# Second graph stage: first maxima in five parts, Exp table earlier, 257 gathered columns, last rows stored from a tile of their own

## The chip, the cores and the metric

The kernel runs on one core of a Trainium2 chip. The core has five engines with instruction streams of their own: TensorE (PE in the profile; PEld is its loading of weights), VectorE (DVE), ScalarE (ACT), GpSimd (POOL) and SyncE (SP), which here only issues DMAs. Each engine takes its instructions in order; between engines semaphores hold an instruction back until what it needs is there. SBUF is the on-chip memory of 128 partitions, PSUM the accumulator memory that TensorE writes, DRAM the large memory. The metric is device time in microseconds (us), the median over runs; lower is better.

## The reference, cut to what matters

Two layers over x of 3327 rows and 256 features, each a graph stage and a feed-forward stage. The first layer is a normalised neighbour sum and a mixture of eight experts. The second layer is graph attention and multi-head attention with four heads and four expert queries each. The graph attention is the part that changes:

```python
Wh = x @ W                                # x: layer-normed rows, 3327 x 256
e_src = Wh @ a[:d_out]
e_dst = Wh @ a[d_out:]
e = jax.nn.leaky_relu(e_src[:, None] + e_dst[None, :], 0.2)
mask = (adj > 0) | jnp.eye(N, dtype=bool)
e = jnp.where(mask, e, NEG_INF)
alpha = jax.nn.softmax(e, axis=1)
h = alpha @ Wh
...
x = x + h
```

## The kernel before

Rows are padded to 3328 = 26 tiles of 128 (NT = 26, P = 128, NP = 3328, HP = 1664). Stages follow one another: `graph0` (first graph), `Experts.run` (experts), `graph1` (second graph), `heads` (attention and everything after it). Inside a stage the order of instructions on each engine is the order in which the program writes them (class InOrder, lines 50 to 99), so a waiting instruction holds all that is written behind it on its engine. Nearly all instructions pass through line 61, so the profile gives that line for them, and they are told apart by the names of their tiles. The SBUF pools of a stage take the space of pools that are closed, and a tile there waits for the last use of what lay there before; a DMA's use ends when it has landed.

`graph1` has two parts.

The first (lines 600 to 618) is a loop over k that takes the 26 row tiles through five steps, each with its own delay: `joined` (VectorE adds the experts' results to x and takes mean and variance, GpSimd makes the scale), `norm` (ScalarE), `turn` (TensorE transposes, ScalarE copies), `project` (TensorE) and `keep` (ScalarE copies to `wh` and `dst`). `gw` holds W and two further columns, W times each half of a, made once in `graph1_weights` (lines 404 to 446). So one matmul gives 258 columns: Wh, e_src, e_dst. `wh` is one tile of 26 times 259 columns, the last column being 1, so that the gathering also gives the softmax's denominator. `dst` holds e_dst plus a bound `shift`, spread over all partitions, 3328 columns.

The maximum of a row's masked e_dst is a product with `sg` (1 for a neighbour, 0 for none) that keeps the largest value: `top` (lines 518 to 528), an instruction on VectorE for each row tile and each part of the columns. PARTS (line 491) gives the bounds: for the first block of four tiles three parts, 1664, 1152 and 512 columns; for later blocks two of 1664. The first part runs inside the loop at k = 18, 20, 22 and 24, the second at k = 28 to 31, the third (line 743) after the loop, once the last tile's `dst` is there. At k = 30 (line 612) ScalarE runs an Exp on one column whose only purpose is to load the table of the exponential; it writes into a column of `own` (line 508), which line 736 then fills.

The second part goes through seven blocks of four row tiles, the last of two, and through 26 column tiles j in each, so 182 steps. `shifts` (line 626) reduces the parts' maxima of a block and makes two vectors a and b; `rows` spreads them by matmuls with ones, `spread_rows` copies them to `bc`. A step is `weights` (VectorE: u = max(a + d8, b); ScalarE: Exp), `masked` (VectorE: p = u where the panel `pan` of the adjacency matrix is set) and `gather` (TensorE: for each row tile, p times `wh[:, j, :]` into an accumulator of 259 columns). Two steps run ahead. In the first 16 steps of a block the next block's rows are turned to signs on ScalarE and their eight maxima taken on VectorE; at j = 16 `shifts` runs for the next block. `finish` (line 717) divides by the denominator, adds to x and stores the row tile to DRAM (`xs`); that DMA is issued by GpSimd. It runs for a block's tiles at the first steps of the next block, for the last block after all steps. GpSimd also sets the diagonal of each block's panel (`noti`, `ident`, line 681). `early` (line 753) runs the first three tiles of the attention's preparation inside the last blocks.

In `heads`, `prepare` and `heads_of` make the keys `kt`, queries `qt` (the first tiles: `qts`), the copy `sxd` and the values for one row tile; `v` and `xt` are tiles of the pool `self.work`, one buffer each. `v` is written to DRAM (`vs`) by four DMAs on SP in `keep_values`, and loaded again as `vr`. `mx` holds the maxima of a unit's scores; `sq` (line 1174) takes an output of ScalarE that is not used, beside the sum that is.

Of the kernel before, what the change touches and what calls it, by code (L numbers as in the profile page):

```python
# [12 lines left out]
F32 = mybir.dt.float32  # L13
BF16 = mybir.dt.bfloat16
# [3 lines left out]
AF = mybir.ActivationFunctionType  # L18
ALU = mybir.AluOpType
AX = mybir.AxisListType  # L20
# [81 lines left out]
class Net:  # L102
# [301 lines left out]
    def graph1_weights(self, pool):  # L404

        a = self.a

        self.gw = pool.tile([P, 2, D + 2], F32, name="gw")
        self.nc.scalar.dma_start(
            out=self.gw[:, :, :D], in_=a["gw"].rearrange("(k p) o -> p k o", p=P)  # L410
        )
        ga = pool.tile([P, 2 * D], F32, name="ga")
        self.nc.scalar.dma_start(out=ga, in_=a["ga"].partition_broadcast(P))
        self.vd = pool.tile([P, 2, P], F32, name="vd")
        self.shift = pool.tile([P, 1], F32, name="shift")
        self.noti = pool.tile([P, P], F32, name="noti")
        junk = pool.tile([P, D], F32, name="pj")

        def make(nc, ps):
            gw, shift = self.gw, self.shift  # L420
            nc.gpsimd.tensor_tensor(self.noti, self.ones, self.ident, ALU.subtract)
            for k in range(2):
                for i in range(2):
                    nc.vector.scalar_tensor_tensor(
                        junk, gw[:, k, :D], 1.0, ga[:, ts(i, D)], ALU.mult, ALU.mult,
                        accum_out=gw[:, k, D + i : D + i + 1],
                    )


            sq = junk[:, :2]  # L430
            nc.vector.tensor_tensor(sq, gw[:, :, D + 1], gw[:, :, D + 1], ALU.mult)
            nc.vector.tensor_copy(
                self.vd, gw[:, :, D + 1 : D + 2].to_broadcast([P, 2, P])
            )
            yield 1
            pv = ps()
            for k in range(2):
                nc.tensor.matmul(
                    pv[:, 0, :1], self.ones, sq[:, k : k + 1], start=(k == 0), stop=(k == 1)
                )  # L440
            nc.vector.tensor_scalar(shift, pv[:, 0, :1], 1e-30, None, ALU.max)
            nc.gpsimd.tensor_tensor(shift, shift, self.nhalf[:, :1], ALU.pow)
            nc.vector.reciprocal(shift, shift)
            nc.vector.tensor_scalar(shift, shift, 16.1, 1.0, ALU.mult, ALU.add)

        return make
# [37 lines left out]
    def graph1(self, xs, vs, made, pool):  # L484
# [3 lines left out]
        self.sxtp, self.sxts = pool, []  # L488
        HP = NP // 2

        PARTS = ((0, HP, HP + 9 * P, NP), (0, HP, NP))
        with ExitStack() as ctx:
            one = ctx.enter_context(tc.tile_pool(name="g1", bufs=1))
            panp = ctx.enter_context(tc.tile_pool(name="g1pan", bufs=3))
# [6 lines left out]
            W = D + 3  # L501
            wh = one.tile([P, NT, W], F32, name="wh")
            nc.gpsimd.memset(wh[:, :, D + 2 : W], 1.0)
            e_src, e_dst = wh[:, :, D], wh[:, :, D + 1]
            dst = one.tile([P, NP], F32, name="dst")
            d8 = one.tile([P, NT], F32, name="d8")
            d2 = one.tile([P, NT], F32, name="d2")
# [9 lines left out]

            def top(t, part, parts):

                if t not in tops:  # L520
                    tops[t] = s.tile([P, 3], F32, tag="gtop", name="gtop", bufs=8)[:, : len(parts) - 1]
                lo, hi = parts[part : part + 2]
                h = lo // HP
                sg = signs[t, h][:, lo - h * HP : hi - h * HP]
                nc.vector.tensor_tensor_reduce(
                    sg, sg, dst[:, lo:hi], 1.0, -3e38, ALU.mult, ALU.max,
                    tops[t][:, part : part + 1],
                )


# [71 lines left out]
            for k in range(NT + 6):  # L602
                if k + 6 < NT:
                    fetch(k + 6)

                for lag, work in ((0, joined), (2, norm), (3, turn), (4, project), (5, keep)):
                    if 0 <= k - lag < NT:
                        work(k - lag)
                for t in range(4):
                    if k == 18 + 2 * t:  # L610
                        top(t, 0, PARTS[0])
                if k == NT + 4:

                    nc.scalar.activation(own[:, 0:1], shift, AF.Exp, scale=-1.0)
                for t in range(4):
                    if k == 28 + t:
                        top(t, 1, PARTS[0])
            first.close()

            ep = ctx.enter_context(tc.tile_pool(name="g1e", bufs=4))  # L620
# [5 lines left out]
            def shifts(b):  # L626


                tiles = blocks[b]
                n, t0 = len(tiles), tiles[0]  # L630
                es = e_src[:, t0 : t0 + n]
                m = s.tile([P, 4], F32, tag="m", name="m")[:, :n]
                ab = s.tile([P, 2, 4], F32, tag="ab", name="ab")[:, :, :n]
                for i, t in enumerate(tiles):
                    nc.vector.tensor_reduce(m[:, i : i + 1], tops.pop(t), AX.X, ALU.max)
                nc.vector.tensor_tensor(m, m, own[:, t0 : t0 + n], ALU.max)
                nc.vector.scalar_tensor_tensor(m, m, shift, es, ALU.subtract, ALU.add)
                nc.vector.scalar_tensor_tensor(m, m, 0.2, m, ALU.mult, ALU.max)
                nc.vector.tensor_tensor(ab[:, 0, :], es, m, ALU.subtract)
                nc.vector.scalar_tensor_tensor(ab[:, 1, :], es, 0.2, m, ALU.mult, ALU.subtract)  # L640
                dg = abp.tile([P, 2, 4, P], F32, tag="dg", name="dg1")
                for i in range(2):
                    (nc.gpsimd if b else nc.vector).tensor_tensor(
                        dg[:, i, :n, :],
                        self.ident.unsqueeze(1).to_broadcast([P, n, P]),
                        ab[:, i, :].unsqueeze(2).to_broadcast([P, n, P]),
                        ALU.mult,
                    )
                return dg
# [57 lines left out]
            def gather(k):  # L707
                b, j = steps[k]
                p = ps_.pop(k)
                for i, t in enumerate(blocks[b]):  # L710
                    if j == 0:
                        accs[t] = psa.tile([P, W], F32, tag="acc", name="acc1")
                    nc.tensor.matmul(
                        accs[t], p[:, i, :], wh[:, j, :], start=(j == 0), stop=(j == NT - 1)
                    )

            def finish(t):
                ph = accs.pop(t)
                rd = s.tile([P, 1], F32, tag="rd", name="rd")
                nc.vector.reciprocal(rd, ph[:, D + 2 : W])  # L720
                nc.vector.scalar_tensor_tensor(
                    x[:, t, :], ph[:, :D], rd, x[:, t, :], ALU.mult, ALU.add
                )
                nc.gpsimd.dma_start(out=xs[ts(t, P), :], in_=x[:, t, :])

            groups = [(b, g) for b in range(len(blocks)) for g in range((NT + 3) // 4)]

# [12 lines left out]
                if k in when:  # L740
                    load(*when[k])
            for t in blocks[0]:
                top(t, 2, PARTS[0])
            spread_rows(0, rows(0, shifts(0)))
            for k in range(3):
                if k in when:
# [178 lines left out]
    def heads(self, xs, vs, out):  # L925
# [3 lines left out]
        with ExitStack() as ctx:  # L929
# [47 lines left out]
            def prepare(t, res):  # L977
# [40 lines left out]
                yield  # L1018

                pp = self.valued(nc, partial(ps.tile, [P, 2, P], F32, tag="b", name="pv"), sxt)  # L1020
                v = self.work.tile([P, D], F32, tag="v", name="v", bufs=1)
                empty(v.rearrange("p (c q) -> p c q", c=2), pp, D)
                yield
                yield from heads_of(t, res, sxt, nz, v)
# [94 lines left out]
            def drain(u, g):  # L1119

                n = span(u["t"], g)[1] * P
                last = g == u["t"] // 4
                if g == 0:
                    u["sc"] = {}
                    u["mx"] = sm.tile([P, 4, 8], F32, tag="mx", name="mx")
                sc = u["sc"][g] = scp.tile([P, 4, BLK], F32, tag="sc", name="sc")
                for e in range(4):
                    s, m = u["pq"][e][:, :n], u["mx"][:, e, g : g + 1]
                    if last:
                        nc.vector.tensor_tensor_reduce(  # L1130
                            sc[:, e, :n], s, mask[:, BLK - n :], 1.0, NEG, ALU.add, ALU.max, m
                        )
                    else:
                        nc.vector.tensor_scalar(
                            sc[:, e, :n], s, 1.0, None, ALU.mult, ALU.max, accum_out=m
                        )
                    load["dve"] += 0.12 + 0.00104 * n
                if last:
                    u["nmax"] = sm.tile([P, 4], F32, tag="nmax", name="anmax")
                    nc.vector.tensor_reduce(  # L1140
                        u["nmax"], u["mx"][:, :, : g + 1], AX.X, ALU.max, negate=True
                    )
                    load["dve"] += 0.2
# [27 lines left out]
                nc.vector.transpose(w, w)  # L1171
                load["dve"] += 0.1 + 0.00417 * n

            sq = one.tile([P, 64], F32, name="sq")


            po = ps_o.tile([P, 4, BLK], F32, tag="po", name="po")
# [973 lines left out]
```

## Time and profile before

Three runs took 2844.63, 2844.79 and 2849.79 us, median 2844.79. One more execution was profiled; it took 2842.88 us, of which 2840.9 lie between the first and the last instruction.

| stretch (us) | what runs | length | PE | DVE | ACT | POOL | PE clock |
|---|---|---|---|---|---|---|---|
| 0 to 69 | first graph: features | 69.0 | 49.3 | 36.6 | 42.4 | 41.6 | 0.97 |
| 69 to 384 | first graph: gathering, routing | 315.0 | 312.6 | 107.5 | 66.9 | 135.8 | 0.99 |
| 384 to 537 | experts | 153.0 | 130.2 | 54.2 | 77.1 | 68.7 | 0.93 |
| 537 to 598.5 | second graph: projecting | 61.5 | 48.5 | 51.3 | 37.2 | 48.2 | 0.87 |
| 598.5 to 611.7 | second graph: up to the first gathering | 13.2 | 3.8 | 7.9 | 5.0 | 0.0 | 0.58 |
| 611.7 to 967.8 | second graph: 182 steps | 356.1 | 323.0 | 340.2 | 191.7 | 89.2 | 0.99 |
| 967.8 to 2840.9 | attention and the rest | 1873.1 | 1786.5 | 1774.4 | 1370.7 | 694.1 | 0.99 |

The columns of the engines give busy time in the stretch; the last column is the clock that TensorE was granted, 1 being full speed. A busy share near the length of a stretch says that the engine may set its pace; what decides is who waits for whom. In lines of the timeline the numbers are start, length, engine, line, operation, output and input tiles, shapes, count, and in brackets how long the engine had stood before it and what ended that. In lines of the chain they are start, length and what held the end of the run there. An fp32 matmul shows as two records.

### The profile page before, as it was taken

How to read it: one execution, taken by the hardware profiler on the slowest of the kernel's cores; microseconds unless marked ns; L12 is line 12 of the kernel's file. 1: busy time of each engine (PE TensorE's matmuls, PEld its weight loads, DVE VectorE, ACT ScalarE, POOL GpSimd, SP SyncE). 2: the span in 40 equal slices, each digit the busy share in tenths (PEclk: the TensorE clock that was granted, in tenths of full speed). 3: DMA queues.
4: the chain of work that ended last, by engine and by line, in shares of the span. 5: the costliest groups of instructions: out<-in, count | busy, mean ns of one | idle time of the engine just before them, and what ended most of it. 6: DMA issues, size and time to landing. Idle time of an engine off the chain costs nothing.

```text
span 2840.9 us, 124987 instructions
## 1 busy us (share of the span) xinstructions
PE 2653.9 (93%) x53422; PEld 1970.7 (69%) x53422; DVE 2372.1 (83%) x5521; ACT 1790.9 (63%) x5131; POOL 1077.6 (38%) x1565
## 2 busy tenths in 40 slices
PE   7999988878988998999999999999999999999995
PEld 5888887756767776676666666666666666666664
DVE  5202643589999798999999999999999999999996
ACT  6520135555555467877777777777778777776774
POOL 5541644532133148655444333333233322223122
PEclk9999999989999899999999999999999999999998
DMA  9994568656785333434434443444434434444432
GB/s 379 386 339 138 191 212 281 202 188 238 277 285 174 94 91 88 117 109 112 119 108 117 118 116 114 119 120 121 115 115 116 126 116 124 123 117 117 116 106 80
DMA packets 257755, 449.29 MB, mean 158 GB/s; under 512 B 58768, under 2 KB 156176, under 8 KB 257072
## 3 DMA queue, kind: packets, MB, share of 16 engines
q1 hardware_dynamic: 245104, 417.11, 47.0%
q0 software_dynamic: 6576, 18.02, 1.7%
q8 instruction: 420, 6.88, 1.0%
q10 hardware_dynamic: 5520, 6.18, 0.6%
q14 instruction: 135, 1.11, 0.1%
HBM read 392.98 MB, written 25.88 MB: 147 GB/s over the span
## 4 chain that ended last, share of the span: by engine, by line
DVE 35%; PE 30%; ACT 4%; issue 2%; POOL 1%; DMA 0%; POOLq 0%; DVEq 0%; ACTq 0%
DVE sc L61 32%; PE pqk L61 11%; PE po L61 10%; PE acc L61 3%; ACT sc L61 2%; PE ptO L61 2%; PE pq L61 1%; PE psxt L61 1%; DVE p L61 1%; PE ph L61 0%; PE pk L61 0%; PE pt L61 0%; DVE sg L61 0%; ACT sq L61 0%; DVE u L61 0%
## 5 line engine op out<-in xcount | busy, mean ns | idle before, releaser
L61 ACT ACTIVATE sc<-sc,anmax 128x512 f32<-128x512 f32 (+3 forms) x1568 | 1041.4, 669 | 101.9 <-DVE anmax L61 101.8
L61 PEld LDWEIGHTS po<-sc,vr 32*64 32x64 f32 x43728 | 659.2, 131 | 300.9 <-issue 149.1
L61 DVE STREAM_TRANSPOSE sc<-sc 128x2048 f32<-128x2048 f32 (+3 forms) x392 | 816.1, 2082 | 11.7 <-ACT sc L61 11.5
L61 PE MATMUL po<-sc,vr 32*64 32x128 f32 x43728 | 758.8, 275 | 32.4 <-DVE sc L61 18.2
L61 PE MATMUL pqk<-kt,qt 64*128 64x512 f32 (+1 forms) x2944 | 764.8, 586 | 19.4 <-DVE fgs L61 7.1
L61 DVE TENSOR_SCALAR_CACHE_REDUCE sc<-pqk 128x512 f32<-128x512 f32 (+2 forms) x1152 | 653.3, 621 | 28.7 <-PE pqk L61 26.7
L61 PEld LDWEIGHTS pqk<-kt,qt 64*128 64x128 f32 x2944 | 315.0, 186 | 240.7 <-issue 85.5
L61 PE MATMUL acc<-wh,p 128*128 128x259 f32 x1352 | 310.9, 387 | 35.3 <-DVE p L61 35.2
L61 PEld LDWEIGHTS acc<-wh,p 128*128 128x128 f32 x1352 | 254.0, 191 | 92.2 <-DVE p L61 51.9
L61 PE MATMUL acc<-y,pan 128*128 128x256 f32 x1352 | 298.4, 382 | 1.7 <-issue 1.7
L61 ACT ACTIVATION_READ_ACCUMULATOR sc<-sc,anmax 128x1 f32 x1568 | 299.5, 191 | 0.0
L61 PEld LDWEIGHTS acc<-y,pan 128*128 128x128 f32 x1352 | 257.2, 191 | 38.7 <-issue 3.3
L61 POOL TENSOR_TENSOR ot<-ot,sxd 128x512 f32<-128x512 f32 x83 | 105.8, 1275 | 435.9 <-ACT ot L61 435.9
L61 DVE CUSTOM_DVE_ANT_0 sc<-pqk,mask 128x512 f32<-128x512 f32 (+3 forms) x416 | 242.0, 636 | 21.1 <-PE pqk L61 20.8
L61 ACT ACTIVATE u<-u,d 128x512 f32<-128x512 f32 (+1 forms) x182 | 125.1, 688 | 156.4 <-DVE u L61 156.2
L61 DVE SCALAR_TENSOR_TENSOR p<-pan,u 128x512 f32<-128x512 f32 (+1 forms) x182 | 127.7, 702 | 11.7 <-PE acc L61 7.3
L61 DVE SCALAR_TENSOR_TENSOR u<-bc,d 128x512 f32<-128x512 f32 (+1 forms) x182 | 136.3, 749 | 0.1
L61 PE MATMUL ptO<-igw,ot 128*128 128x68 f32 x832 | 116.1, 283 | 4.3 <-DVE sc L61 2.1
L61 ACT COPY qkv<-ptO 128x272 f32<-128x272 f32 x104 | 39.7, 382 | 126.7 <-PE ptO L61 126.6
L61 PEld LDWEIGHTS ptO<-igw,ot 128*128 128x128 f32 x832 | 101.8, 193 | 23.1 <-issue 15.2
L61 ACT ACTIVATE junk<-ar 128x1664 bf16<-128x1664 f32 x52 | 82.8, 1592 | 54.3 <-DMA ar<-in_adj_dram 53.7
L61 DVE CUSTOM_DVE_ANT_0 sg<-sg,dst 128x1664 bf16<-128x1664 bf16 (+2 forms) x56 | 100.7, 1806 | 1.2 <-ACT dst L61 1.0
(366 smaller groups left out, 3074.6 us busy)
## 6 DMA issues: line engine op xcount, KB each, us to landing
vr<-vs SPq DMA_DIRECT2D x976, 128.0 KB
ar<-in_adj_dram SPq DMA_DIRECT2D x104, 832.0 KB
vr<-vs SPq DMA_DIRECT2D x544, 96.0 KB
pan<-in_adjt_dram SPq DMA_DIRECT2D x156, 256.0 KB
pan<-in_adjt_dram SPq DMA_DIRECT2D x26, 1024.0 KB
pan<-in_adjt_dram SPq DMA_DIRECT2D x20, 832.0 KB
w1e<-w SPq DMA_DIRECT2D x59, 256.0 KB
took<-places SPq DMA_DIRECT2D x59, 129.0 KB
```

The source lines that it names most:

```text
L61: made = make(*args, **kw)
```

## The change

The maxima of the first block are taken in five parts of 1664, 1152, 256, 128 and 128 columns. The third and fourth run at k = 31, the loop's last turn, behind the second part of the fourth tile; the fifth is where the third was. The parts' maxima of a block's four tiles share one tile, so that one reduction takes the place of four (of two in the last block). The Exp that loads the table stands at k = 20 and writes into a tile of its own.

In `gw` and `wh` the two columns of e_src and e_dst move ahead of Wh, so that Wh and the column of ones lie side by side; the gathering takes 257 columns from the third on, and its accumulators are 257 wide.

`finish` writes the two tiles of the last block into tiles `end` of their own, in a pool that stays open, instead of back into x; their two DMAs are issued by ScalarE instead of GpSimd.

In the attention stage `v` shares the one slot of `xt`, `mx` has three buffers instead of four, and `sq` is bf16 instead of fp32.

```diff
-            out=self.gw[:, :, :D], in_=a["gw"].rearrange("(k p) o -> p k o", p=P)
+            out=self.gw[:, :, 2:], in_=a["gw"].rearrange("(k p) o -> p k o", p=P)
...
-                        junk, gw[:, k, :D], 1.0, ga[:, ts(i, D)], ALU.mult, ALU.mult,
-                        accum_out=gw[:, k, D + i : D + i + 1],
+                        junk, gw[:, k, 2:], 1.0, ga[:, ts(i, D)], ALU.mult, ALU.mult,
+                        accum_out=gw[:, k, i : i + 1],
...
-        PARTS = ((0, HP, HP + 9 * P, NP), (0, HP, NP))
+        PARTS = ((0, HP, HP + 9 * P, HP + 11 * P, HP + 12 * P, NP), (0, HP, NP))
...
-            e_src, e_dst = wh[:, :, D], wh[:, :, D + 1]
+            e_src, e_dst = wh[:, :, 0], wh[:, :, 1]
...
-                if t not in tops:
-                    tops[t] = s.tile([P, 3], F32, tag="gtop", name="gtop", bufs=8)[:, : len(parts) - 1]
+                b, i = t // 4, t % 4
+                if b not in tops:
+                    tops[b] = s.tile([P, 4, 5], F32, tag="gtop", name="gtop", bufs=3)[
+                        :, :, : len(parts) - 1
+                    ]
...
-                    tops[t][:, part : part + 1],
+                    tops[b][:, i, part : part + 1],
...
-                if k == NT + 4:
-
-                    nc.scalar.activation(own[:, 0:1], shift, AF.Exp, scale=-1.0)
+                if k == 20:
+
+                    nc.scalar.activation(s.tile([P, 1], F32, tag="gpre", name="gpre", bufs=1), shift, AF.Exp, scale=-1.0)
...
+                if k == 31:
+                    for part in range(2, 4):
+                        for t in range(4):
+                            top(t, part, PARTS[0])
...
-                for i, t in enumerate(tiles):
-                    nc.vector.tensor_reduce(m[:, i : i + 1], tops.pop(t), AX.X, ALU.max)
+                nc.vector.tensor_reduce(m, tops.pop(b)[:, :n, :], AX.X, ALU.max)
...
-                        accs[t] = psa.tile([P, W], F32, tag="acc", name="acc1")
+                        accs[t] = psa.tile([P, D + 1], F32, tag="acc", name="acc1")
                     nc.tensor.matmul(
-                        accs[t], p[:, i, :], wh[:, j, :], start=(j == 0), stop=(j == NT - 1)
+                        accs[t], p[:, i, :], wh[:, j, 2:W], start=(j == 0), stop=(j == NT - 1)
...
-                nc.vector.reciprocal(rd, ph[:, D + 2 : W])
+                nc.vector.reciprocal(rd, ph[:, D : D + 1])
+                end = x[:, t, :]
+                if t in blocks[-1]:
+                    end = pool.tile([P, D], F32, tag="end", name="end", bufs=2)
                 nc.vector.scalar_tensor_tensor(
-                    x[:, t, :], ph[:, :D], rd, x[:, t, :], ALU.mult, ALU.add
-                )
-                nc.gpsimd.dma_start(out=xs[ts(t, P), :], in_=x[:, t, :])
+                    end, ph[:, :D], rd, x[:, t, :], ALU.mult, ALU.add
+                )
+                (nc.scalar if t in blocks[-1] else nc.gpsimd).dma_start(out=xs[ts(t, P), :], in_=end)
...
-                top(t, 2, PARTS[0])
+                top(t, 4, PARTS[0])
...
-                v = self.work.tile([P, D], F32, tag="v", name="v", bufs=1)
+                v = self.work.tile([P, D], F32, tag="xt", name="v", bufs=1)
...
-                    u["mx"] = sm.tile([P, 4, 8], F32, tag="mx", name="mx")
+                    u["mx"] = sm.tile([P, 4, 8], F32, tag="mx", name="mx", bufs=3)
...
-            sq = one.tile([P, 64], F32, name="sq")
+            sq = one.tile([P, 64], BF16, name="sq")
```

More of the change, by code (lines that the diff above doesn't have):

```diff
@@ L424, in make @@
                     nc.vector.scalar_tensor_tensor(
-                        junk, gw[:, k, :D], 1.0, ga[:, ts(i, D)], ALU.mult, ALU.mult,
-                        accum_out=gw[:, k, D + i : D + i + 1],
+                        junk, gw[:, k, 2:], 1.0, ga[:, ts(i, D)], ALU.mult, ALU.mult,
+                        accum_out=gw[:, k, i : i + 1],
                     )
             sq = junk[:, :2]
-            nc.vector.tensor_tensor(sq, gw[:, :, D + 1], gw[:, :, D + 1], ALU.mult)
+            nc.vector.tensor_tensor(sq, gw[:, :, 1], gw[:, :, 1], ALU.mult)
             nc.vector.tensor_copy(
-                self.vd, gw[:, :, D + 1 : D + 2].to_broadcast([P, 2, P])
+                self.vd, gw[:, :, 1:2].to_broadcast([P, 2, P])
             )
```

## The prediction

> **What bounds the kernel now.** I read the page's chain first, then the timeline around the two ends of the second graph stage, then the waits inside it. The span is 2840.9 us. From 970 us on it is the attention stage, in which VectorE (DVE) and TensorE (PE) share the chain; the change leaves its arithmetic alone.
>
> ```profile
> DVE sc L61 32%; PE pqk L61 11%; PE po L61 10%; PE acc L61 3%; ACT sc L61 2%; PE ptO L61 2%; PE pq L61 1%; PE psxt L61 1%; DVE p L61 1%; PE ph L61 0%; PE pk L61 0%; PE pt L61 0%; DVE sg L61 0%; ACT sq L61 0%; DVE u L61 0%
> ```
>
> So what can be had lies in three places between 545 and 972 us. The first is the seam between projecting the rows (to 598 us) and the first gathering (from 611.67). In VectorE's timeline (start, length, operation, repeat count, idle before it and its releaser):
>
> ```profile
> 594.98 0.08 DVE L61 DVE_READ_ACCUMULATOR2_ANT gtop<- 128x1 f32 x1
> 598.08 0.27 DVE L61 TENSOR_SCALAR d<-wh 128x26 f32<-128x26 f32 x2 [3.03 <-ACT wh L61]
> 600.03 0.24 DVE L61 TENSOR_SCALAR own<-wh,shift 128x26 f32<-128x26 f32 x1 [1.68 <-ACT own L61]
> 600.19 0.69 DVE L61 CUSTOM_DVE_ANT_0 sg<-sg,dst 128x512 bf16<-128x512 bf16 x1
> 602.63 0.34 DVE L61 TENSOR_REDUCE m<-gtop 128x1 f32<-128x3 f32 x4
> 603.01 0.16 DVE L61 TENSOR_TENSOR m<-m,own 128x4 f32<-128x4 f32 x1
> ```
>
> and in ScalarE's (ACT):
>
> ```profile
> 598.12 0.37 ACT L61 ACTIVATE dst<-pd,shift 128x128 f32<-128x128 f32 x1
> 598.50 1.28 ACT L61 ACT_TABLE_LOAD   x1
> 599.79 0.20 ACT L61 ACTIVATE own<-shift 128x1 f32<-128x1 f32 x1
> ```
>
> VectorE stands 3.03 us for the last projected row, then 1.68 us because the early Exp, behind its table load, writes a column of `own`, which VectorE must write next; then come four maxima of 512 columns and four reductions. All this stands on the path to the first gathering.
>
> Second, the gathering from 612 to 967 us: VectorE is busy 53.4 to 54.4 us of the 55 to 56 of each of the first three blocks and waits for TensorE 0.6 to 0.8 us in each; only the end is TensorE's. Third, the seam to the attention stage, in the chain of waits:
>
> ```profile
> 967.46 0.57 POOL xs L61
> 968.06 2.31 DMA xs<-x
> 970.58 0.38 ACT kt L61
> 971.00 0.60 ACT qts L61
> 971.96 0.51 PE pqk L61 x4
> ```
>
> The new stage's `kt` lies where `x` lay, and waits for the last rows of `x` to reach DRAM.
>
> **Maxima in five parts, and the table load.** The path from the last row's copy to the block's maximum now is: two scalings at 598.08, `own` free at once, the last four maxima over 128 columns, one reduction. Maxima start 0.61 us apart at 512 columns (600.19 to 602.63 holds four) and 1.28 us at 1152, so about 0.075 us and 1.05 ns a column: 0.34 us at 256, 0.21 at 128; in the attention stage the same operation over 128 columns does start 0.21 us apart. The last four need `dst` of tile 25, ready at 598.49, so they start near 598.6 and end at 599.45. One reduction in place of four takes 0.19 instead of 0.38 us. `m` starts at 599.64 instead of 603.01: **3.4 us** less, and what follows (products with the identity, two matmuls, two copies) is unchanged.
>
> The eight maxima put ahead take 4 x 0.34 + 4 x 0.21 = 2.2 us, inside the 3.03 us in which VectorE stood. Those over 256 columns can start at 595.06; those over 128 need tile 24's `dst`, ready at 596.58, and end by 597.45, 0.6 us before the cover ends. Without the cover they cost 2.2 us. Beside them GpSimd (POOL) masks diagonals of the first panel: 0.45 us an operation when VectorE stands, 1.45 to 1.58 beside maxima. It ended at 598.2; even with all 2.2 us added it is done by 600.4, and the first mask needs it near 607.5.
>
> The table load moves to k = 20, after ScalarE's `dst` of tile 15 (573.90). It costs 1.28 + 0.20 = 1.48 us there, and ScalarE stands 0.75 and 1.54 us before its next two rows for GpSimd: nothing. VectorE next waits for ScalarE at 588.6. Identity, Copy and Sign run later without another load (none after 598.5), so none comes back. Between the bounds of the whole part, 1.7 us (only the wait for `own` goes) and 5.3 (3.4 and, if the two broadcast matmuls ran in the 1.88 us of a later block instead of 3.75, 1.9 more), I take 3.4, the row's.
>
> [...]
>
> TensorE's clock over this seam:
>
> ```profile
> 598.00:600.00 2.00, 0.08 (x1) 0.00 (x0) 0.27 (x2) 1.90 (x4) 0.19 (x1) 1.00 0.00 0
> 600.00:602.00 2.00, 0.00 (x0) 0.00 (x0) 1.97 (x6) 0.00 (x0) 0.00 (x0) 0.66 0.00 0
> 602.00:604.00 2.00, 0.00 (x0) 0.00 (x0) 1.83 (x14) 0.00 (x0) 0.00 (x0) 0.50 0.00 0
> ```
>
> (bounds, length, busy time of PE, its loads, DVE, ACT, POOL, then granted clock.) A mean of 0.66 of 1.0 and 0.5 puts the fall near 600.64; the broadcast matmuls, from 604.7 to about 601.3, stay behind it, so they stay slow.
>
> [...]
>
> **One reduction a block.** The maxima of blocks 1 to 5 are reduced in the middle of the block before, in a stretch that VectorE sets:
>
> ```profile
> 814.88 0.33 DVE L61 TENSOR_REDUCE m<-gtop 128x1 f32<-128x2 f32 x4
> 815.24 0.16 DVE L61 TENSOR_TENSOR m<-m,own 128x4 f32<-128x4 f32 x1
> ```
>
> 0.36 us becomes some 0.18 (the fourth alone is 0.14 long): 5 x 0.18 = **0.9 us**. The last block's falls where TensorE sets the pace: 0.
>
> **257 columns.** A gathering record (two to a matmul) starts every 218.6 ns at 259 columns (20.99 us for 96 in the chain); the first graph's, at 256, every 215.1 (465 in 100 us). So 1.2 ns a column, 2.4 ns a record. It counts only where TensorE sets the pace: the last 250 records (911.9 to 966.9), 0.6 us, and about 45 a block before VectorE next waits for it, 5 x 0.11: **1.1 us**. Bounds: 0.6 and all 1352 x 2.4 = 3.2 us. I take the row of waits, nearer the lower.
>
> **Last rows by ScalarE.** `kt` no longer waits for a DMA, only for VectorE's last read of `x` (967.75), as `pk` does (967.94). `pk` ends near 968.7, `pq` at 969.67; so `kt` runs at 968.85, `qts` at 969.75, and `pqk` starts near 970.7 instead of 971.96: **1.25 us**. GpSimd loses two DMA issues (1.15 us) that nothing waits for. ScalarE gains two, 0.34 to 1.05 us each in its rows at the start, waiting for VectorE at 967.2 and 967.75; behind them stand `kt`, `qts` and `sx`, and they are over by 968.8, or 969.9 at the dearest, where `qts` then slips 0.5. Bounds: 0 (something else holds `kt`) and 2.0 (970.58 less 968.6). The rows are next read near the end: no wait.
>
> **Room made for it.** `v` takes the slot of `xt`, so a tile's `xt` copy waits until the last tile's four writes from `v` have landed. Closest are tiles 3 and 4: issued by 1017.99, 2.31 us to land as `xs`, 1020.3, against the copy at 1024.10: 3.8 us of cover; later tiles have 29 us or more. Without cover a copy stands up to 4.3 us. `mx` in three buffers is written and read by VectorE alone, and `sq` in bf16 is a discarded output: 0 each.
>
> **Sum.** 3.4 + 0.9 + 1.1 + 1.25 = 6.65 us. Against the profiled execution (2842.88 us, 1.98 outside its span) that is 2836.2; the median shown, 2844.79, is 1.9 higher, so **2838.1 us** for a median. What a measurement can tell from no change is 0.2%, 5.7 us: the forecast stands just beyond it.
>
> **Rivals.** *The clock helps*: 1.9 us more, 2836.2; for it the pause halved, against it the fall at 600.64. 0.10. *The first seam's gain is swallowed*: loads or signs hold the first block, 2841.5. Against it: VectorE never waits more than 0.4 us at a time in 612 to 667, and the loads are started by the computing and shift with it. 0.12. *`kt` is held by something else*, 2839.4: the chain names only the last release, though `pk` passes at 967.94. 0.13. *It doesn't do what it says*, the gains hidden throughout: 2844.8, 0.05. *Slower*: the `xt` copy, in order on ScalarE ahead of the exponentials, waits for `v`'s writes in each of 23 preparations. From 6.65/23 = 0.29 us each the gain is gone; at 0.6 us each, 13.8, the time is 2852. For it: those writes queue on SP behind value loads; against it the cover of 3.8 and 29 us. It decides once SP is four us later at 1015. 0.05.
>
> **How the numbers follow.** The forecast has 0.55, its own range 2835.5 to 2839.6; 0.10 of it lies above 2839.1, the bound of faster. Faster: 0.45 + 0.10 = 0.55. Same: 0.10 + 0.12 + 0.13 + 0.05 = 0.40. Slower: 0.05. The range for 8 in 10 goes from 2834.0 (clock and the upper column price) to 2843.0 (only part of the seams).
>
> **What would show it.** `own` with no idle before it; the last maxima 128 wide; `m` 1.5 us after the `d` pair; one reduction a block; 217 ns a record before 966; `kt` before 969 with no DMA ahead. What would make it wrong: the `d` pair held by the maxima ahead of it, a ScalarE wait before `xt`, or a gathering that starts 3.4 us earlier and yet ends where it did.

## The result, and the profile after

| kernel | median us | runs | lowest to highest | ratio to before, 95% interval |
|---|---|---|---|---|
| before | 2844.71 | 10 | 2842.65 to 2849.79 | |
| after | 2852.81 | 10 | 2849.39 to 2857.23 | 1.0025 [1.0015, 1.0034] |

The change makes the kernel slower by a quarter of a per cent: 7.1 us of 2844.7 by the ratio, 8.1 by the medians. The prediction had 2838.1 us and gave "slower" one chance in twenty. The profiled execution after has a span of 2850.9 us, 10.0 more than before. The span, cut at the same instructions in both profiles, in us:

| stretch | before | after | difference |
|---|---|---|---|
| start to the last of the 1152-wide maxima (593.44 and 606.92) | 593.4 | 606.9 | +13.5 |
| from there to the first gathering record (611.67 and 622.60) | 18.2 | 15.7 | -2.6 |
| first to last gathering record | 354.8 | 352.7 | -2.1 |
| last gathering record to the first `pqk` (971.96 and 979.21) | 5.5 | 3.9 | -1.6 |
| first `pqk` to the end | 1868.9 | 1871.7 | +2.8 |

The three stretches that the prediction worked on gave 6.2 us (the shown differences are rounded), against its 6.65. The loss lies ahead of them all, in stages for which the prediction counted nothing. The last row, +2.8, is within what one execution differs from another there: the stage as it was before took 1868.9 us here and 1870.2 to 1879.7 in six other profiles of this study, the changed one 1871.7 here and 1866.4 to 1872.6 in six others.

First the lines that answer to those of before. The chain by lines, of the page after:

```profile
DVE sc L61 30%; PE pqk L61 11%; PE po L61 11%; PE acc L61 3%; PE ptO L61 2%; ACT sc L61 2%; DVE p L61 1%; DMA pan<-in_adjt_dram 1%; PE pq L61 1%; DVE sg L61 1%; PE psxt L61 1%; DVE u L61 1%; DMA ar<-in_adj_dram 1%; PE ph L61 1%; PE pt L61 0%
```

Two entries are new against before: DMAs of the column panels `pan` and of the row tiles `ar`. They are no sign of the loss. The chain after is followed back only to 749 us, so these are transfers of the second graph, and the page of `home`, an experiment below that is faster than before, has DMA `pan` at 1% too. The chain says nothing of the first graph in either page; its waits have to be read directly.

VectorE after, at the seam between projecting and gathering (start, length, operation):

```profile
608.46 0.67 DVE L61 CUSTOM_DVE_ANT_0 sg<-sg,dst 128x256 bf16<-128x256 bf16 x1
...
612.44 0.26 DVE L61 TENSOR_SCALAR d<-wh 128x26 f32<-128x26 f32 x2
612.62 0.23 DVE L61 TENSOR_SCALAR own<-wh,shift 128x26 f32<-128x26 f32 x1
612.77 0.28 DVE L61 CUSTOM_DVE_ANT_0 sg<-sg,dst 128x128 bf16<-128x128 bf16 x1
...
613.73 0.17 DVE L61 TENSOR_REDUCE m<-gtop 128x4 f32<-128x20 f32 x1
613.94 0.16 DVE L61 TENSOR_TENSOR m<-m,own 128x4 f32<-128x4 f32 x1
```

The two waits of before, 3.03 us for the last row and 1.68 for the Exp, are gone; no idle time is left in brackets. From the `d` pair to the block's maximum it is 1.50 us (612.44 to 613.94), 4.93 before. Later blocks have the single reduction too; in VectorE's timeline after, ahead of the fifth of the seven blocks:

```profile
824.78 0.15 DVE L61 TENSOR_REDUCE m<-gtop 128x4 f32<-128x8 f32 x1
824.96 0.16 DVE L61 TENSOR_TENSOR m<-m,own 128x4 f32<-128x4 f32 x1
```

And ScalarE's timeline after, at the seam to the attention stage:

```profile
976.05 0.94 ACTq L61 DMA_DIRECT2D xs<-end  x2
977.58 0.37 ACT L61 COPY kt<-pk 128x256 f32<-128x256 f32 x1 [5.21 <-PE pk L61]
978.56 0.60 ACT L61 ACTIVATE qts<-pq 128x512 f32<-128x512 f32 x1 [0.60 <-PE pq L61]
```

`kt` now waits for TensorE's `pk` and not for a DMA; the two stores that ScalarE issues end at 976.99, before `pk` does.

Now the first graph, 69 to 396 us, for which the prediction counted nothing. TensorE's timeline from 55 to 400 us, before (its first line with `acc`):

```profile
69.63 199.35 PE L61 MATMUL acc<-y,pan 128*128 128x256 f32 x910 [1.71 <-issue]
```

and after:

```profile
70.10 50.23 PE L61 MATMUL acc<-y,pan 128*128 128x256 f32 x224 [1.71 <-issue]
121.05 7.14 PE L61 MATMUL acc<-y,pan 128*128 128x256 f32 x32 [0.71 <-DMA pan<-in_adjt_dram]
...
208.93 74.06 PE L61 MATMUL acc<-y,pan 128*128 128x256 f32 x334 [3.97 <-DMA pan<-in_adjt_dram]
```

Before, TensorE goes through 910 records without a pause. After, it starves for a panel eleven times, 10.2 us together; the gathering's last record comes at 395.5 us instead of 381.5, for a start only 0.5 us later. The other 3.3 us of the 13.5 are in the records themselves: TensorE is busy with them for 301.7 us on the page after, 298.4 before. The bytes moved are the same (449.29 MB in both pages), so the stream itself must be slower. The DMA view of 130 to 180 us shows where: 40 slices of 1.25 us, GB/s in each. Before:

```profile
GB/s 426 396 340 348 409 427 426 366 348 365 414 424 421 349 346 372 347 415 424 336 348 394 423 426 392 335 349 445 426 426 347 342 338 348 346 370 386 365 373 372
```

After:

```profile
GB/s 386 315 292 344 387 415 390 327 292 320 393 426 399 323 301 327 395 373 416 341 304 295 297 422 426 367 315 290 349 408 421 380 312 292 348 412 405 390 313 299
```

SyncE issues two row tiles and a panel in turn, and the rate swings with them. The tops, some 425 GB/s, are the same in both rows. The bottoms fall from some 345 to some 295, by 15%. One of the two kinds of transfer has become slower. Means of the 50 us: 381 before, 355 after. From 174 us on the row of before also holds loads of the experts' weights, which after come from 184 us on; in 85 to 120 us, ahead of them, the means are 388 and 355.

### The profile page after: what moved, and what is told of

Same layout as the page of the kernel before. It is cut to its first block, busy times and chain, and to the rows that moved or that the text cites. A ratio compares the mean times of both kernels' runs of the same rounds, so it can differ in the third digit from the quotient of the medians.

```text
span 2850.9 us, 124990 instructions
## 1 busy us (share of the span) xinstructions
PE 2651.8 (93%) x53422; PEld 1968.5 (69%) x53422; DVE 2372.8 (83%) x5518; ACT 1789.5 (63%) x5131; POOL 1076.9 (38%) x1563
## 2 busy tenths in 40 slices
DMA packets 257948, 449.29 MB, mean 158 GB/s; under 512 B 58769, under 2 KB 156433, under 8 KB 257265
## 4 chain that ended last, share of the span: by engine, by line
DVE 35%; PE 31%; ACT 3%; issue 2%; DMA 2%; POOL 1%; SPq 0%; DVEq 0%; POOLq 0%; ACTq 0%
DVE sc L61 30%; PE pqk L61 11%; PE po L61 11%; PE acc L61 3%; PE ptO L61 2%; ACT sc L61 2%; DVE p L61 1%; DMA pan<-in_adjt_dram 1%; PE pq L61 1%; DVE sg L61 1%; PE psxt L61 1%; DVE u L61 1%; DMA ar<-in_adj_dram 1%; PE ph L61 1%; PE pt L61 0%
## 5 line engine op out<-in xcount | busy, mean ns | idle before, releaser
L61 PE MATMUL acc<-wh,p 128*128 128x257 f32 x1352 | 307.8, 385 | 36.4 <-DVE p L61 36.3
L61 PE MATMUL acc<-y,pan 128*128 128x256 f32 x1352 | 301.7, 383 | 11.9 <-DMA pan<-in_adjt_dram 10.2
L61 DVE CUSTOM_DVE_ANT_0 sc<-pqk,mask 128x512 f32<-128x512 f32 (+3 forms) x416 | 241.9, 636 | 20.6 <-PE pqk L61 20.3
L61 DVE CUSTOM_DVE_ANT_0 sg<-sg,dst 128x1664 bf16<-128x1664 bf16 (+3 forms) x64 | 102.6, 1618 | 1.2 <-ACT dst L61 1.0
```

Source lines behind the costliest of these rows:

```text
L61: made = make(*args, **kw)
```

## What could make a stream slower that nobody edited

The two kernels issue the same transfers in the first graph. What differs is where they land. The pool `small` (line 107) is opened right behind the constants, ahead of every stage's pools. In it the old `gtop` took eight tiles of 32 bytes, 256 in all; the new one takes three of 96 bytes and the new `gpre` 32, so 320. Every tile behind that pool moved up by 64 bytes a partition: `pan` from byte 105728 to 105792, `ar` from 138496 to 138560. The old addresses are multiples of 256, the new ones are 64 past one. A panel is written in runs of 512 bytes (a run is bytes that lie side by side in one partition), a row tile in runs of 6656.

The theory, which no run had shown so far: a run that lies off a multiple of 256 touches a 256-byte piece more, three for two in a panel (half as many again), 27 for 26 in a row tile (4% more). So `pan` pays and `ar` doesn't, and any remainder costs alike. The rivals: the new order of instructions itself; the move of 64 bytes whatever its remainder; `ar` as the culprit; a cost that grows with the remainder, as wasted bytes would; and addresses in the attention stage, whose tiles moved too.

## The experiments

Ratios are to runs of the kernel before on the same chip.

**home**: the whole change, with the pool `small` as long as before, so that all tiles up to the second graph lie where they lay.

```diff
-tops[b] = s.tile([P, 4, 5], F32, tag="gtop", name="gtop", bufs=3)[
+tops[b] = s.tile([P, 4, 5], F32, tag="gtop", name="gtop", bufs=2)[
...
-nc.scalar.activation(s.tile([P, 1], F32, tag="gpre", name="gpre", bufs=1), shift, AF.Exp, scale=-1.0)
+nc.scalar.activation(s.tile([P, 16], F32, tag="gpre", name="gpre", bufs=1)[:, :1], shift, AF.Exp, scale=-1.0)
```

> The changed kernel with the pool of small tiles brought back to its old length (the maxima in two buffers instead of three, the early Exp's tile 64 bytes): x, ar, pan and all tiles up to the attention stage lie at the addresses of the kernel before; in the attention stage they stay shifted. Theory P (place): the changed kernel's loss is the 64 bytes by which the growth of that pool moved the panels and rows of the first graph off multiples of 256 bytes, so that their DMAs run slower; then the first graph's gathering ends near 381 us again instead of 395, its panel waits are gone, and the time is 2844.7 - 6 = 2838 to 2841 us. Rival E (edits): one of the edits themselves slows the first stage or the attention; then it stays at 2852 +- 2. Rival C (chip): the difference is of executions; then it falls anywhere, with the kernel before moving along.

**home_heads**: `home`, and 96 unused bytes in the attention stage behind `sq`, so that `vr`, `sxd`, `v` and `xres` lie on multiples of 256.

```diff
             sq = one.tile([P, 64], BF16, name="sq")
+            one.tile([P, 24], F32, name="room2")
```

> As the one before, and 96 bytes more ahead of the attention stage's tiles, so that vr, sxd, v and xres, too, start at multiples of 256 bytes (160 beyond one in the kernel before this run, 32 in the kernel before, 224 in the changed one). Theory P carried on to the attention stage: the 2.8 us which that stage lost between 32 and 224 come back and a little more, 2 to 4 us below the kernel home. Rival: the attention stage is not held by its DMAs, then it equals home within 1.5 us.

**g0_64** and **g0_256**: the kernel before, with 64 or 256 unused bytes ahead of the first graph's panels; nothing else of the change.

```diff
             panp = ctx.enter_context(tc.tile_pool(name="g0pan", bufs=4))
+            panp.tile([P, 16], F32, tag="room", name="room", bufs=1)
```

(`[P, 64]` in `g0_256`.)

> The kernel before with 64 unused bytes ahead of pan in the first graph's pools and nothing else: pan and ar of that stage start 64 bytes beyond a multiple of 256, every other tile stays where it was. Theory P: the first graph's gathering ends near 395 us, panel waits of some 10 us appear, time 2844.7 + 10 to 14 = 2855 to 2859 us. Rivals E and C: no change, 2843 to 2847 us.

> The kernel before with 256 unused bytes at the same place: pan and ar move further than in g0_64, but to multiples of 256 again. Theory P (the remainder by 256 decides): no change, 2843 to 2847 us. Rival D (any other place is worse, through banks or overlaps): as slow as g0_64.

| kernel | median us (runs) | before beside it | ratio, 95% interval | first graph's last record | GB/s in 130 to 180 us |
|---|---|---|---|---|---|
| home | 2839.30 (12) | 2845.56 (29) | 0.9979 [0.9967, 0.9991] | 381.2 | 381 |
| home_heads | 2838.38 (12) | 2845.56 | 0.9975 [0.9963, 0.9986] | 380.4 | 383 |
| g0_64 | 2858.39 (6) | 2845.56 | 1.0042 [1.0026, 1.0059] | 392.2 | 354 |
| g0_256 | 2843.98 (12) | 2845.56 | 0.9990 [0.9978, 1.0002] | 380.7 | 382 |

64 bytes alone, without any edit of the change, cost 0.42%; 256 bytes cost nothing. And the change without the 64 bytes is 0.21% faster than before. So the order of instructions isn't the cause, and neither is a move as such. The waits of TensorE between 69 and 400 us in `g0_64` (time, times, longest) name the same releaser as after, which has 10.2 us there:

```profile
PE acc L61 <- DMA pan<-in_adjt_dram: 9.3, 12, 3.8
```

`home_heads` can't be told from `home`: the intervals overlap almost wholly, and its attention took 1872.6 us against 1869.2. The addresses there (32 past a multiple before, 224 after, 160 in `home`, 0 in `home_heads`) cost nothing that these runs show.

**g0_pan64** and **g0_ar64**: the two kinds of tile apart. The first moves the panels by 64 bytes and gives the row tiles 192 more, so that these stay on a multiple; the second moves the row tiles alone.

```diff
             panp = ctx.enter_context(tc.tile_pool(name="g0pan", bufs=4))
+            panp.tile([P, 16], F32, tag="room", name="room", bufs=1)
...
             rowp = early.enter_context(tc.tile_pool(name="g0row", bufs=6))
+            rowp.tile([P, 48], F32, tag="room", name="room", bufs=1)
```

(`g0_ar64`: the second only, with `[P, 16]`.)

> The kernel before with only the panels pan of the first graph 64 bytes off; ar at a multiple of 256. pan is written in runs of 512 bytes, 2 pieces or 3 when off. Theory T: nearly all of the loss, 2854 to 2859 us. Rival B: 40% of it, 2849 to 2852 us.

> The kernel before with only the rows ar of the first graph 64 bytes beyond a multiple of 256; pan stays on one. A row of ar is one run of 6656 bytes, 26 pieces of 256 bytes or 27 when it starts off a multiple. Theory T (touched pieces of 256 bytes: a run costs as many as it touches): 4% more of ar's share, the time within 2845 to 2848 us. Rival B (moved bytes: all bytes that land off a multiple cost the same): ar has 1.7 MB of the 2.7 MB a column tile while both stream, so 60% of the loss of 13 us, 2851 to 2855 us.

**g0_128** and **g0_224**: as `g0_64`, with 128 and 224 bytes.

```diff
             panp = ctx.enter_context(tc.tile_pool(name="g0pan", bufs=4))
+            panp.tile([P, 32], F32, tag="room", name="room", bufs=1)
```

(`[P, 56]` in `g0_224`.)

> pan and ar of the first graph 128 bytes beyond a multiple of 256. Theory T: as many pieces are touched as at 64, the same loss, 2856 to 2860 us. Rival S (the bytes between the multiple and the start are moved too, so the loss grows with the remainder): twice the added part, 2866 to 2872 us. Rival A (multiples of 128 are enough): no loss, 2843 to 2847 us.

> pan and ar of the first graph 224 bytes beyond a multiple of 256. Theory T: the same loss as at 64, 2856 to 2860 us. Rival S: 3.5 times the added part, above 2880 us.

| kernel | median us (runs) | before beside it | ratio, 95% interval | first graph's last record | GB/s in 130 to 180 us |
|---|---|---|---|---|---|
| g0_pan64 | 2857.97 (10) | 2848.12 (25) | 1.0034 [1.0024, 1.0045] | 392.7 | 357 |
| g0_ar64 | 2844.78 (10) | 2848.12 | 0.9998 [0.9982, 1.0013] | 380.8 | 384 |
| g0_128 | 2860.87 (6) | 2848.12 | 1.0043 [1.0026, 1.0060] | 394.8 | 356 |
| g0_224 | 2859.71 (8) | 2848.12 | 1.0039 [1.0028, 1.0050] | 395.3 | 356 |

The panels carry the loss, the row tiles none. The DMA view of the same 50 us shows it burst by burst, for `g0_pan64`:

```profile
GB/s 292 351 415 426 379 318 294 312 394 426 401 346 291 338 402 394 395 335 300 325 410 415 403 336 297 318 400 426 410 335 300 311 388 421 419 351 304 297 290 295
```

and for `g0_ar64`:

```profile
GB/s 421 421 353 345 382 425 421 413 342 329 415 428 426 370 346 353 392 432 421 364 348 379 409 426 421 337 348 408 427 426 381 350 333 348 345 361 384 373 372 374
```

The bottoms are mostly at 290 to 300 where the panels lie off a multiple and at 330 to 350 where only the row tiles do.

The traces also hold the time of each packet of a DMA, and here a packet is a run. Up to 215 us a packet of 512 bytes took 27.1 ns on average before and in the four kernels with the panels on a multiple (`home`, `home_heads`, `g0_256`, `g0_ar64`). It took 31.3 ns after, 30.9 in `g0_pan64`, and 31.5, 31.7 and 32.4 in `g0_64`, `g0_128` and `g0_224`. A packet of 6656 bytes has a median of 253 ns before and of 253 in `g0_ar64`, 64 bytes past a multiple. The 26 panels are 53248 packets; 4.2 ns more for each, over the 16 DMA engines of the page, is an estimate of 13.9 us, beside the 13.5 that the stage lost.

And 64, 128 and 224 bytes past a multiple cost the kernel the same (1.0042, 1.0043, 1.0039, with wide overlap), and the parts added to a packet are 4.4, 4.6 and 5.3 ns over the 27.1. That is how a count of touched pieces would have it, three for two whatever the remainder, and not how wasted bytes would: their part would be 3.5 times as large at 224 as at 64. The size does not fit the count alone: half as many again would be 41 ns a packet, and 31 to 32 were measured. So the remainder is shown as the cause; why it costs what it costs stays open, a count of pieces or another cost that is nearly fixed for each run of bytes with a ragged start or end.

**The parts of the change one by one**, each undone in `home`, with a profile and one time. `home_3parts`: three parts for the first block, nothing at k = 31.

```diff
-        PARTS = ((0, HP, HP + 9 * P, HP + 11 * P, HP + 12 * P, NP), (0, HP, NP))
+        PARTS = ((0, HP, HP + 9 * P, NP), (0, HP, NP))
...
-                if k == 31:
-                    for part in range(2, 4):
-                        for t in range(4):
-                            top(t, part, PARTS[0])
...
-                top(t, 4, PARTS[0])
+                top(t, 2, PARTS[0])
```

> The kernel home with the first block's maxima in three parts again (512 columns after the loop). From the last copy to wh to the first gathering it was 14.0 us in the kernel before and 11.4 in home. The prediction's step says the parts are worth 4 x (0.61 - 0.21) = 1.6 us: 13.0 us here. The rival, that the eight maxima put ahead hold the scalings and give part of it back (they took 0.60 us each at 256 columns where 0.34 was reckoned): less, 12.0 to 12.6 us. Single times differ by some 2 us, the stretch is to be read, not the time.

`home_late`: the Exp that loads the table at k = 30 again, still in its own tile.

```diff
-                if k == 20:
+                if k == NT + 4:
```

> The kernel home with the early Exp at k = 30 again, in its own tile (so own no longer waits for it). The prediction's step says the wait for own was the cost, not ScalarE's time: the stretch from the last copy to wh to the first gathering stays at 11.4 us. Rival: the table load itself holds the path through ScalarE (dst, copies): 12 us or more.

`home_259`: the gathering takes all 259 columns.

```diff
-                        accs[t] = psa.tile([P, D + 1], F32, tag="acc", name="acc1")
+                        accs[t] = psa.tile([P, W], F32, tag="acc", name="acc1")
...
-                        accs[t], p[:, i, :], wh[:, j, 2:W], start=(j == 0), stop=(j == NT - 1)
+                        accs[t], p[:, i, :], wh[:, j, :], start=(j == 0), stop=(j == NT - 1)
...
-                nc.vector.reciprocal(rd, ph[:, D : D + 1])
+                nc.vector.reciprocal(rd, ph[:, D + 2 : W])
...
-                    end, ph[:, :D], rd, x[:, t, :], ALU.mult, ALU.add
+                    end, ph[:, 2 : D + 2], rd, x[:, t, :], ALU.mult, ALU.add
```

> The kernel home with 259 columns a gathering again (the two scalar columns ahead of Wh, the accumulators 259 wide). First to last gathering record took 354.8 us before and 353.0 in home, where one reduction a block is reckoned at 0.9 of it and the two columns at 1.1. Here 354.1 +- 0.3 us. Rival: the columns are hidden, 353.0.

`home_noend`: the last rows go back into x and are stored by GpSimd.

```diff
-                if t in blocks[-1]:
-                    end = pool.tile([P, D], F32, tag="end", name="end", bufs=2)
...
-                (nc.scalar if t in blocks[-1] else nc.gpsimd).dma_start(out=xs[ts(t, P), :], in_=end)
+                nc.gpsimd.dma_start(out=xs[ts(t, P), :], in_=end)
```

> The kernel home with the last two row tiles written back into x and stored by GpSimd. From the last gathering record to the first matmul of the attention's scores it was 5.5 us before and 3.9 in home. Here 5.5 us, with kt behind the DMA of xs again. Rival: kt is held by something else and the gain is another edit's: 3.9.

| kernel | one time, us | span | first 1152-wide maximum to first gathering | gathering | last gathering record to `pqk` |
|---|---|---|---|---|---|
| before | 2842.88 | 2840.9 | 22.1 | 354.8 | 5.5 |
| home | 2836.77 | 2834.9 | 19.5 | 353.0 | 3.9 |
| home_3parts | 2838.07 | 2836.2 | 20.3 | 353.0 | 3.9 |
| home_late | 2834.85 | 2833.0 | 19.5 | 353.0 | 3.9 |
| home_259 | 2841.28 | 2839.4 | 19.5 | 353.9 | 3.9 |
| home_noend | 2836.70 | 2834.8 | 19.5 | 353.0 | 5.6 |

A single time can't settle a difference of one or two us (the runs of `home` lie between 2835.85 and 2846.53), so these kernels are read by their stretches alone. (The times of before and `home` are those of their profiles above; run beside the other four, before took 2844.14.) In these executions each stretch returns what its own part had brought: 0.8 us for the five parts, 0.9 for the columns, 1.8 for the last rows. Whether the 1.8 are kept to the end is not shown: the attention of `home_noend` was 2.8 us shorter than that of `home`, and the two times are alike. The Exp's place costs nothing: from the first maximum to `m`, VectorE's sequence lasts 10.85 us in `home` (589.31 to 600.16) and 10.85 in `home_late` (588.21 to 599.06). I measure that seam from the first maximum and not, as the expectations did, from the last projected row, because in these runs the moment of that row went with the clock that TensorE was granted (6.4 us after the first maximum at 1.00, 7.8 to 8.1 behind a stretch at 0.50 to 0.56, below). By the expectations' own measure `home_3parts` took 12.3 us, which is the rival's range, and `home_late` 13.1, which taken alone would be the rival's too; but `home_259`, with the Exp at k = 20, also took 13.1. In `home_late` the clock stayed at 1.00 between 594 and 596 us, where before and `home` had 0.50, the row came earlier, and VectorE wasn't ready for it.

So what the seam gains depends on when that row comes. From the first maximum to the first gathering all six profiles with five parts take 19.5 us. The seven with the seam of before take 20.2 to 22.1, 21.2 on average: the last row's copy starts 6.4 us after the first maximum in three of them (`g0_64`, `g0_256`, `g0_ar64`) and 7.8 to 8.1 in the other four, before among them. In the three the granted clock was 1.00 up to the row; in the four it was 0.50 to 0.56 for a stretch of 2 us shortly ahead of it. Where the row comes early, VectorE stands less for it; in `g0_64`:

```profile
608.57 0.44 DVE L61 TENSOR_SCALAR d<-wh 128x26 f32<-128x26 f32 x2 [1.35 <-ACT wh L61]
```

The 2.6 us between the profiles before and after are thus the top of a range that begins at 0.7; on average it is 1.7. The five parts by themselves may bring nothing on average. `home_3parts`, whose row came late (8.1 us), takes 12.3 us from the row's copy to the gathering; with the row at 6.4 us that makes an estimate of 18.7 us, 0.8 less than with five parts, where with the late row it is 0.8 more. No run shows three parts with an early row.

Why the five parts bring less than forecast is in VectorE's timeline of `home`:

```profile
594.69 0.66 DVE L61 CUSTOM_DVE_ANT_0 sg<-sg,dst 128x256 bf16<-128x256 bf16 x1
...
597.07 0.53 DVE L61 CUSTOM_DVE_ANT_0 sg<-sg,dst 128x128 bf16<-128x128 bf16 x1
...
598.66 0.26 DVE L61 TENSOR_SCALAR d<-wh 128x26 f32<-128x26 f32 x2
...
600.16 0.16 DVE L61 TENSOR_TENSOR m<-m,own 128x4 f32<-128x4 f32 x1
```

and in that of `home_3parts`:

```profile
598.39 0.27 DVE L61 TENSOR_SCALAR d<-wh 128x26 f32<-128x26 f32 x2 [3.03 <-ACT wh L61]
598.58 0.24 DVE L61 TENSOR_SCALAR own<-wh,shift 128x26 f32<-128x26 f32 x1
598.83 0.69 DVE L61 CUSTOM_DVE_ANT_0 sg<-sg,dst 128x512 bf16<-128x512 bf16 x1
...
601.60 0.16 DVE L61 TENSOR_TENSOR m<-m,own 128x4 f32<-128x4 f32 x1
```

In `home` the eight maxima put ahead run from 594.69 to 598.66, 3.97 us instead of the 2.2 worked out: 0.60 each at 256 columns (594.69 to 597.07 holds four), 0.40 on average at 128. The last row's copy had ended at 597.76, so the `d` pair started 0.9 us after the row was there (2.6 us after it in the changed kernel, where the row came early). In `home_3parts` that pair waits for the row alone.

## Why the prediction was wrong, and where it was right

**The step that failed** is "Room made for it". It priced `v`, `mx` and `sq` by asking who would wait for a slot, and asked nothing of what the new tiles do to the addresses of all that is allocated behind them; its first part held that "what can be had lies in three places between 545 and 972 us", and no rival looked ahead of them. So the growth of the pool `small` stood in the sum at nothing, without a reason. The 64 bytes put the first graph's panels off a multiple of 256, and that stage lost 13.5 us. Could it have been asked? The sizes were there: eight small tiles became three larger ones and one more, in a pool that lies ahead of every stage. So was the risk: the page of before has the DMA engines busy over nine tenths in the first three slices, 213 us. The price was in no row of before.

**The slower rival** was another one: the `xt` copy did not wait for `v`'s writes. ScalarE's waits ahead of its 23 `xt` copies name no DMA; they are for TensorE's `pt` above all, 24.1 us in nine waits before and after alike. That this rival's time of 2852 us lies beside the 2852.81 measured is chance. The attention stage of `home`, which has that shared slot, the three `mx` and the bf16 `sq`, lasted 1869.2 us against 1868.9.

**Maxima in five parts, and the table load**: forecast 3.4 us, measured 2.6 (18.2 less 15.7 after, 22.1 less 19.5 in `home`), and 1.7 on average over the profiles of both seams. From the `d` pair to `m` the forecast holds, 1.50 us against 1.56 worked out. The term that was mis-sized is that of the eight maxima, 3.97 us for 2.2, and with it the cover: 0.6 us to spare became 0.9 too few in `home` and 2.6 after. The cover itself, 3.03 us, was that of one execution; in the seven profiles with that seam it is 1.35 to 3.03. The prediction had the held `d` pair at its end, among what would make it wrong. The table load costs nothing at either place, as forecast (10.85 us from the first maximum to `m` in `home` and in `home_late`); what the old place cost was VectorE's wait for the column of `own`. `home_3parts` keeps 1.7 of the 2.6 us, from that wait and the single reduction, and the parts bring the other 0.8.

**One reduction and 257 columns**: forecast 0.9 + 1.1 = 2.0, measured 2.1 after and 1.8 in `home` (354.8 less 353.0), of which `home_259` gives 0.9 to the columns.

**Last rows by ScalarE**: forecast 1.25, measured 1.6; `home_noend` returns 1.8. ScalarE's two DMA issues took 0.94 us together and held nothing.

**The other rivals.** The clock didn't help: TensorE after was granted 0.63 between 612 and 614 us and 0.50 between 614 and 618, and the two broadcast matmuls took 3.75 us as before. Nor was TensorE's pause ahead of them halved, as the rival had it: 5.76 us after, 6.65 before. No run shows at which length of pause the clock would have stayed up. The seam's gain was swallowed in part only, by the maxima; `kt` was held by nothing else.

**The sum**: 6.65 us forecast for the parts, 6.2 measured after, or 5.4 with the seam at its average. Where the addresses are put back, the kernel takes 0.9979 of before [0.9967, 0.9991], 6.0 us by the ratio, and its median of 2839.3 us lies 1.2 above the number predicted. The rest is the 64 bytes: 1.0025 over 0.9979 is 0.46%, 13 us, and `g0_64` alone shows 0.42%. `home` is the version to keep: faster than before by 0.21%, and by these ratios than after by the same 0.46% (the two were not run side by side).

## What to carry to other kernels

A tile that grows in a pool opened early moves everything behind it: before costing an edit at nothing, work out the new addresses of the tiles that DMAs fill, and look at the stages whose DMA engines are busy, edited or not. Where short runs (512 bytes here) stream in and set the pace, keep their tile on a multiple of 256 bytes (27 ns a packet here, against 31 to 32 off one); a few unused bytes do it. And time a small instruction from a row in which the same neighbour works beside it, not from one in which that neighbour stands (0.60 us a maximum here, for the 0.34 worked out); and take a wait that is to cover other work from more than one execution.

## What the runs showed of the hardware

**Where a DMA wrote in SBUF set the rate of runs of 512 bytes.** Runs of 512 bytes landing 64, 128 or 224 bytes past a multiple of 256 took 31 to 32 ns a packet against 27 on a multiple, and went at some 295 GB/s in their bursts against some 345; runs of 6656 bytes, 64 past one in `g0_ar64`, kept their median of 253 ns and the bursts near 425. The second graph's panel had moved by 64 bytes too after, and cost nothing that shows, in a stretch in which TensorE stands 36.3 us for VectorE's `p` (the page after): 352.7 us of gathering against 353.0 in `home`.

**VectorE's maxima and GpSimd's masks took longer beside each other.** In `home` a maximum over 128 columns starts 0.21 us after the one before where GpSimd stands, and at 0.46 mostly while it masks a panel; one over 256 took 0.60. A mask took 0.45 or 0.46 us in `home_3parts`, where VectorE stood, and 0.50 to 0.63 in `home`. GpSimd's timeline in `home` over the same time:

```profile
595.03 0.63 POOL L61 TENSOR_TENSOR pan<-pan,noti 128x128 f32<-128x128 f32 x1
595.74 0.52 POOL L61 TENSOR_TENSOR pan<-pan,ident 128x128 f32<-128x128 f32 x1
596.22 0.63 POOL L61 TENSOR_TENSOR pan<-pan,noti 128x128 f32<-128x128 f32 x1
```

Two masks start in 1.19 us (595.03 to 596.22), and two maxima in 1.19 (two of 0.595), and the starts alternate: maxima at 594.69, 595.28, 595.88 and 596.47, masks at 595.03, 595.74 and 596.22. The prediction had applied such a slowing to GpSimd's side only. No run took the masks away, so that they slow the maxima rests on these moments and on the 0.21 us without them; why they do is not shown.
